# A conditioned mixture-of-experts layer: the gate folded into the second layer, the shared expert's turns deferred, and the pages' first layer with the expert's weights as stationary operand

## Chip, cores and metric

The kernel runs on one core of a Trainium2 chip. The metric is the device time of one execution in microseconds; the time before is the median of three runs. A profiled execution of the same kernel gives the span (first to last instruction) and everything that is read from the profile.

## What is computed

`x` has 8 batches of 512 tokens of 256 float32 numbers, here called tokens throughout. The reference, cut to what matters (`_ln` is a layer norm with gain and offset):

```python
h = _ln(x, pw_g[pathway], pw_b[pathway])            # gain and offset gathered by token
h = _ln(h, cp_g[compartment], cp_b[compartment])
t = _ln(x, tm_g[time], tm_b[time])
m, n, r = (x + mlp_ln(state) for each of three states of the batch)
s = _ln(x, ms_g[scale], ms_b[scale])
cat = concatenate([w[0]*h, w[1]*t, w[2]*m, w[3]*n, w[4]*r, w[5]*s])     # 6 x 256
xf = _ln(silu(cat @ int_W1 + int_b1) @ int_W2 + int_b2, int_g, int_be)  # 256
probs = softmax(xf @ gate_w.T)                      # 16 experts, the best 4 are used
moe = sum over the best 4 of p * (silu(xf @ w1[e].T) * (xf @ w3[e].T)) @ w2[e].T   # hidden width 128
shared = (silu(xf @ sw1.T) * (xf @ sw3.T)) @ sw2.T
out = x + moe + shared
```

## The kernel before

The work has two stages. **Stage 1** goes through the batches, each of 4 tiles of 128 tokens. Per batch: the gathers of `pw` rows and the first normalisation; transposes of x and of the normalised x (`turn_x`) and of h (`turn_h`); factors that select a class's gain by a product with a one-hot matrix (`factor`); the first layer into `ph` (`hidden`, L744 to L757, two halves of 128 hidden numbers, four sources in the order of the list HIDDEN) and its silu (`hidden_a`); the second layer into `pz` (`raw`, L766 to L780, two tiles in one PSUM buffer); statistics straight from PSUM (`raw_d`, `z_stats`); then

- `z_norm` (L803): ScalarE normalises from PSUM into `z`, tokens on the partitions;
- `z_turn` and `z_turn_a` (L807, L819): TensorE transposes z, ScalarE applies the norm's gain and offset and writes `xf` with the features on the partitions;
- `gate` (L827): xf tiles are the stationary operand, the 16 gate columns stream;
- `choose` (L840): VectorE takes the four largest of 16 logits; `rank` (L859): TensorE counts each token's place within its expert; `place` (L882): VectorE makes slot numbers from that;
- `scatter` (L946): one indirect DMA from GpSimd for each tile and each of the four choices writes rows of z into their slots of `xs_d` in HBM;
- `shared_1` and `shared_2` (L599 to L628): the shared expert from xf, with silu on ScalarE and a product and an addition to `x_all` on VectorE.

The last batch does the steps from `z_norm` to `place` in two groups of two tiles. `page_owners` and `page_experts` (L968 to L989) then find the expert of each page.

**Stage 2** goes through 143 pages of 128 slots each, sorted by expert, in 72 pairs (loop L1333 to L1362). For pair i: `load` brings four pages at a time from `xs_d`; `turn` (L1243, matmuls at L1250) transposes the pages, and ScalarE applies gain and offset (L1255); `first` (L1265): each page's transposed tokens are the stationary operand and the expert's w1 and w3, 256 columns at a place given by a register, stream (L1271); silu on ScalarE, product g on VectorE; `second_t` (L1283, matmuls at L1287) transposes g, VectorE copies it to `at`; `second` (L1295, L1304): at is stationary, w2 streams; ScalarE copies the result `yo`, and SP stores it into `ys_d`. `experts` (L1230) loads the numbers of four pages' experts into registers of TensorE. `fetch` (L1194) gathers results by slot from `ys_d` on GpSimd, at most two per pair; `weigh` adds them with their weights on VectorE, and `pick_weights` finds these weights during the first 32 pairs.

**What sets the order.** The class Plan (L61 to L126) is a list scheduler: every step is added with its engine, an estimated length, a rank, the steps that it follows, and slots that it takes and gives back (for instance two PSUM buffers each of the kinds t, h, m and o, three z buffers, six xf buffers). It writes each engine's order, which is then kept; the smallest rank that can start goes first. The shared expert has rank 400 plus its batch, so it fills what is left. GpSimd's transfers are kept in the program's order (`in_turn`), and scatters and gathers are paced by steps of VectorE (`in_time`). Stage 2's order is that of its loop. SP's order is that of the planned loads, then loads, stores and output of stage 2.

Of the kernel before, what the change touches and what calls it, by code (L numbers as in the profile page):

```python
# [18 lines left out]
P = 128  # L19
# [20 lines left out]
K_H, K_T, K_M, K_N, K_R, K_S = range(6)  # L40

F_B2, F_H, F_T, F_S = range(4)
F_X = F_B2
# [86 lines left out]
def adaln_ffn_kernel(ctx: ExitStack, tc: tile.TileContext, a: dict, out: bass.AP):  # L130
# [112 lines left out]
    iw2 = const.tile([P, NC, D], F32)  # L243
    gw = const.tile([P, NC, E], F32)
    ident = const.tile([P, P], F32)
# [18 lines left out]
    cls16 = const.tile([P, 4, D], BF16)  # L264
# [40 lines left out]

    iws = const.tile([P, 4, NC, D], F32)
    bias_t = const.tile([P, NC, B], F32)

    if True:
# [4 lines left out]
        def load_rest():  # L314
            nc.sync.dma_start(out=iw2, in_=a["int_W2"])
            nc.sync.dma_start(out=gw, in_=a["gate_w"])

# [48 lines left out]
        def halves(h):  # L366
            k = slice(F_T, F_S + 1) if h == 0 else slice(F_B2, F_H + 1)
            return cls16[:, k], second[:, k], tab[:, k]
# [38 lines left out]

        def gpsimd_tables():
            nc.gpsimd.memset(before, 1.0 / P)
# [46 lines left out]
        made = {}  # L456

# [141 lines left out]
    def shared_1(b, i):  # L599

        xf = res[b]["xf"]
        if i == 0:
            res[b]["act"] = p3.tile([P, S], F32, tag=tag("sact", "sh", b, 0), name=f"sact_{b}")
        ph = res[b]["sh", i] = ps_h.tile([P, S], F32, tag=tag("h", "sh", b, 0, i=i), name=f"sh{i}_{b}")
        for c in range(NC):
            nc.tensor.matmul(ph, s13[:, c, i], xf[:, c, :], start=(c == 0), stop=(c == NC - 1))  # L606
# [23 lines left out]
    with (  # L630
# [45 lines left out]
        def layer1_d(b, j):  # L676
# [4 lines left out]
            if "st_h" not in res[b]:  # L681
                res[b]["st_h"] = p2.tile([P, NJ, 6], F32, tag="st_h", name=f"st_h_{b}", bufs=B)
# [59 lines left out]
        HIDDEN = (F_T, F_S, F_X, F_H)  # L742

        def hidden(b, m, q):  # L744

            k = HIDDEN[q]
            cols = slice(m * P, (m + 1) * P)
            if q == 0:
                if m == 0:
                    res[b]["hid"] = p2.tile([P, NC, S], F32, tag=tag("hid", "hid", b, 0, 0), name=f"hid_{b}")  # L750
                res[b]["ph", m] = ps_h.tile([P, S], F32, tag=tag("h", "hid", b, m, 0), name=f"ph_{b}_{m}")
# [9 lines left out]
        def hidden_a(b, m):  # L761
            nc.scalar.activation(  # L762
# [3 lines left out]
        def raw(b, jj):  # L766

            hid = res[b]["hid"]
            if jj == 0:
                res[b]["z"] = p2.tile([P, NJ, D], F32, tag=tag("z", "raw", b, 0), name=f"z_{b}")  # L770
                res[b]["st_z"] = p2.tile([P, NJ, 6], F32, tag="st_z", name=f"st_z_{b}", bufs=B)
            pz = res[b]["pz", jj] = ps_o.tile([P, 2, D], F32, tag=tag("o", "raw", b, jj), name=f"pz_{b}_{jj}")
            for i in range(2):
                j = 2 * jj + i
                js = slice(j * P, (j + 1) * P)
                nc.tensor.matmul(
                    pz[:, i, :], hot_t[b][0:KCLS, js], cls16[0:KCLS, F_B2, :], start=True, stop=False
                )
                for m in range(NC):
                    nc.tensor.matmul(  # L780
                        pz[:, i, :], hid[:, m, js], iw2[:, m, :], start=False, stop=(m == NC - 1)
                    )

        def raw_d(b, jj):
            for i in range(2):
                vector.bn_stats(res[b]["st_z"][:, 2 * jj + i, :], res[b]["pz", jj][:, i, :])
# [16 lines left out]
        def z_norm(b, g, j):  # L803
            rs, nb = res[b]["zn", g]
            normalize(res[b]["z"][:, j, :], res[b]["pz", j // 2][:, j % 2, :], rs, nb, j - tiles_of(b, g)[0])
# [21 lines left out]
        def gate(b, g):  # L827
            xf, js = res[b]["xf"], tiles_of(b, g)
            pg = res[b]["pg", g] = ps_m.tile([P, len(js), E], F32, tag=tag("m", "gate", b, g), name=f"pg_{b}_{g}")
            for i, j in enumerate(js):  # L830
                for c in range(NC):
                    nc.tensor.matmul(  # L832
                        pg[:, i, :],
                        xf[:, c, j * P : (j + 1) * P],
                        gw[:, c, :],
                        start=(c == 0),
                        stop=(c == NC - 1),
                    )

        def choose(b, g):  # L840
# [4 lines left out]
            vector.tensor_copy(lx[:, js_, 0:E], res[b]["pg", g])  # L845
# [35 lines left out]

        def place(b, g):  # L882
# [4 lines left out]
            pr, mask = res[b]["pr", g], mask_all[:, b, js_]  # L887
# [5 lines left out]


            up = t("up")
            vector.tensor_scalar(up, pr[:, n:], 0.5 - 0.5 / P, ROUND, ALU.add, ALU.add)
            vector.tensor_scalar_add(end1, up, -ROUND)
# [33 lines left out]
            vector.tensor_tensor(pos, pr[:, 0:n], end0, ALU.is_ge)  # L931
            vector.tensor_mul(pos, pos, step)
            vector.tensor_add(pos, pos, pr[:, 0:n])
# [12 lines left out]
        def scatter(b, j, k):  # L946
# [3 lines left out]
                in_=res[b]["z"][:, j, :],  # L950
# [79 lines left out]
        add("rest", on="SP", took=0.9, rank=-94, lag=land, do=load_rest)  # L1030
# [6 lines left out]
        add("open", on="SP", took=0, rank=60, after=[("bias", 0), ("bias", 1), ("sca", 2), ("fill", 2)] + [("wown", i) for i in range(3)], do=open_weights)  # L1037
# [29 lines left out]
        add("wx", on="POOL", took=5, rank=-2, after=[("wsoft",), ("int", 1)], do=setup_x)  # L1067
        add("s1", on="PE", took=2, rank=-4, takes=["m"], after=[("st",)], do=states_1)
# [13 lines left out]
        for b in range(B):  # L1082
# [14 lines left out]
            for k in (F_T, F_S, F_H):  # L1097
                for c in range(NC):
# [7 lines left out]
                        gives=[("m", ("f", b, k, c))], do=factor_d)  # L1106
# [7 lines left out]
            for m in range(NC):  # L1114
                for q, k in enumerate(HIDDEN):
# [4 lines left out]
                    gives = {F_T: ("cat", ("f", b, F_T, 0)), F_S: ("cat", ("f", b, F_S, 0)), F_X: ("catx", ("tx", b, 0)), F_H: ("cath", ("f", b, F_H, 0))}  # L1120
                    add("hid", b, m, q, on="PE", took=1.75 + 0.22 * (k == F_H), rank=t + 20 + 7 * m, after=need,
                        takes=(["h"] + ["hid"] * (m == 0)) * (q == 0), gives=[gives[k]] * m, lag=0.12 if q == 3 else 0.0, do=hidden)
                add("hida", b, m, on="ACT", took=0.6, rank=t + 20 + 7 * m, after=[("hid", b, m, 3), ("bias", m)], gives=[("h", ("hid", b, m, 0))], do=hidden_a)
            for jj in range(2):
                add("raw", b, jj, on="PE", took=1.95, rank=t + 35 + jj, after=[("hida", b, m) for m in range(NC)] + [("begun", ("raw", b, 0))] * jj,
                    takes=["o"] + ["z"] * (jj == 0), gives=[("hid", ("hid", b, 0, 0)), ("hot", ("ht", b))] * jj, do=raw)
                add("rawd", b, jj, on="DVE", took=0.9, rank=t + 35 + jj, after=[("raw", b, jj)], do=raw_d)
            GROUPS = range(2 if b == B - 1 else 1)
            for g in GROUPS:
                js = tiles_of(b, g)  # L1130
                part = len(js) / NJ
                add("zs", b, g, on="DVE", took=2.4, rank=t + 26, after=[("rawd", b, j // 2) for j in js[::2]], do=z_stats)
                for j in js:
                    add("zn", b, g, j, on="ACT", took=0.49, rank=t + 27 + 0.1 * j, after=[("zs", b, g)], gives=[("o", ("raw", b, j // 2))] * (j % 2), do=z_norm)
                for c in range(NC):
                    add("zt", b, g, c, on="PE", took=0.44 * part, rank=t + 29 + c, after=[("zn", b, g, j) for j in js] + [("begun", ("zt", b, 0, 0))] * (c + g > 0),
                        takes=["t"] + ["xf"] * (c + g == 0), do=z_turn)
                    add("xf", b, g, c, on="ACT", took=0.2 + 0.48 * part, rank=t + 29 + c, after=[("zt", b, g, c)], gives=[("t", ("zt", b, g, c))], do=z_turn_a)
                add("gate", b, g, on="PE", took=1.8 * part, rank=t + 32, after=[("xf", b, g, c) for c in range(NC)], takes=["m"], do=gate)
                add("ch", b, g, on="DVE", took=0.5 + 1.6 * part, rank=t + 33, after=[("gate", b, g), ("tables",)], gives=[("m", ("gate", b, g))], do=choose)  # L1140
                add("rank", b, g, on="PE", took=0.5, rank=t + 34, after=[("ch", b, g), ("tables",)] + ([("pl", b, 0)] if g else [("pl", b - 1, 0)] if b else []), takes=["m"], do=rank)
                add("pl", b, g, on="DVE", took=4.0 + 2.2 * part, rank=t + 34, after=[("rank", b, g)] + [("po", (b - 4) // 2)] * (b >= 4), gives=[("m", ("rank", b, g))], lag=0.6, do=place)
                for j in js:
                    for k in range(TOPK):
                        add("sc", b, j, k, on="POOL", took=POOL_STEP, rank=t + 50 + 0.1 * j + 0.01 * k, after=[("pl", b, g), ("fill", b)],
                            gives=[("z", ("raw", b, 0))] * ((j, k) == (NJ - 1, TOPK - 1)), lag=2.3, do=scatter)
            for i in range(2):
                add("sh", b, i, on="PE", took=1.72, rank=400 + b, after=[("begun", ("sh", b, 0))] * i + [("xf", b, g, c) for g in GROUPS for c in range(NC)] + [("sw",)],
                    takes=["h", "h", "sact"] * (i == 0), do=shared_1)
            add("sha", b, on="ACT", took=0.6, rank=t + 50, after=[("sh", b, 0)], do=shared_1a)  # L1150
            add("shd", b, on="DVE", took=0.6, rank=t + 51, after=[("sha", b), ("sh", b, 1)], gives=[("h", ("sh", b, 0))], do=shared_1d)
            for jj in range(2):
                add("so", b, jj, on="PE", took=0.86, rank=400.5 + b, after=[("shd", b)] + [("begun", ("so", b, 0))] * jj, takes=["o"],
                    gives=[("xf", ("zt", b, 0, 0)), ("sact", ("sh", b, 0))] * (jj == 1), do=shared_2)
                add("sod", b, jj, on="DVE", took=0.68, rank=t + 60, after=[("so", b, jj)], gives=[("o", ("so", b, jj))], do=shared_2d)
# [67 lines left out]

    def load(q):
# [196 lines left out]
```

## Time and profile before

| what | us |
|---|---|
| median of three runs (555.72 to 556.39) | 555.81 |
| profiled execution, its own time | 556.97 |
| its span | 555.3 |
| TensorE busy | 512.4 |
| VectorE busy | 376.9 |
| GpSimd busy | 294.8 |
| ScalarE busy | 256.7 |
| first raw of batch 0 begins | 54.74 |
| last raw of batch 7 ends, about | 256.8 |
| last scatter begins | 297.25 |
| first transposes of the pages begin | 305.60 |
| a pair of pages, start to start | 3.25 |

Times within the profile are counted from the start of the span. PE is TensorE's matmuls and PEld its loads of the stationary operand, which overlap the matmuls; DVE is VectorE, ACT ScalarE, POOL GpSimd, SP the engine that issues most DMAs. A line of the timeline gives the start, the time from the first start to the last end, the engine, the source line, the operation with its output and inputs, and in brackets the idle time before it with what ended it. VectorE's operations go through a helper and all carry L139.

### The profile page before, as it was taken

The page shows a single profiled execution, that of the slowest core. Times are in us where ns is not written, and L with a number is a line of the kernel's source. Part 1 is how long each engine was busy: PE and PEld are TensorE (multiplying, and loading weights), DVE is VectorE, ACT ScalarE, POOL GpSimd, SP SyncE. Part 2 cuts the span into 40 slices and gives each one's busy share as a digit, 9 for nine tenths or more (in the row PEclk, how much of TensorE's full clock was granted, in tenths as well). Part 3 has the DMA queues.
Part 4 walks back from the last instruction along what each step waited for, and adds up shares of the span by engine and source line. Part 5 has one row for each costly group of instructions (what it writes and reads, how often), then busy time and mean ns, then how long its engine had stood idle before and what let it go on. Part 6 is the DMA issues. An engine that isn't in the chain of part 4 may idle for free.

```text
span 555.3 us, 8874 instructions
## 1 busy us (share of the span) xinstructions
PE 512.4 (92%) x2487; PEld 368.5 (66%) x2487; DVE 376.9 (68%) x1469; ACT 256.7 (46%) x509; POOL 294.8 (53%) x319
## 2 busy tenths in 40 slices
PE   3899999999989999998888999999999999999980
PEld 2446656554646555655545888888888888888860
DVE  8889889897868989857663534566664454455452
ACT  5552734451615532322102655655565556556640
POOL 7602207656656667575673002555655566665663
PEclk9998999998989999999899999999999999999995
DMA  6975657962879356646224355788888898888764
GB/s 220 368 215 157 185 169 211 259 205 94 264 224 301 122 161 220 182 152 224 87 104 158 108 173 169 220 292 264 264 257 260 249 273 280 262 261 254 225 200 120
DMA packets 107612, 116.83 MB, mean 210 GB/s; under 512 B 8744, under 2 KB 95141, under 8 KB 107565
## 3 DMA queue, kind: packets, MB, share of 16 engines
q1 hardware_dynamic: 92398, 74.26, 42.8%
q0 software_dynamic: 14848, 41.96, 24.9%
q8 instruction: 21, 0.34, 0.3%
q14 instruction: 26, 0.21, 0.1%
q10 hardware_dynamic: 319, 0.05, 0.1%
HBM read 57.78 MB, written 58.46 MB: 209 GB/s over the span
## 4 chain that ended last, share of the span: by engine, by line
PE 80%; DVE 11%; ACT 3%; DMA 3%; issue 2%; POOL 1%; POOLq 0%; DVEq 0%
PE hp L1271 22%; PE ph L757 17%; PE yo L1304 11%; PE xt L1250 6%; PE sh L606 4%; PE pz L780 3%; PE so L622 3%; PE pa L1287 3%; PE pg L832 2%; PE ptx L705 2%; PE pf L716 2%; DMA pw<-in_pw_dram,idx 1%; PE pth L732 1%; DVE cat L139 1%; PE p_table L395 1%
## 5 line engine op out<-in xcount | busy, mean ns | idle before, releaser
L1198 POOL DMA_INDIRECT yg<-ys_d,slot_all x128 | 124.1, 970 | 125.8 <-ACT yo L1308 43.5
L947 POOL DMA_INDIRECT xs_d<-z,slot_all x128 | 126.3, 986 | 78.0 <-issue 22.2
L1271 PE MATMUL hp<-w,xtt 128*128 x572 | 135.5, 380 | 0.2 <-ACT xtt L1255 0.2
L1271 PEld LDWEIGHTS hp<-w,xtt 128*128 128x128 f32 x572 | 103.1, 190 | 11.6 <-ACT xtt L1255 0.6
L139 DVE TENSOR_TENSOR g<-g,hp 128x256 f32<-128x256 f32 x72 | 30.2, 419 | 103.7 <-ACT g L1279 103.7
L757 PE MATMUL ph<-cat,iws 128*128 128x512 f32 x192 | 92.8, 613 | 0.0
L1255 ACT ACTIVATE xtt<-xt,vecs 128x256 f32<-128x256 f32 x144 | 73.2, 560 | 3.0 <-PE xt L1250 2.8
L1304 PE MATMUL yo<-w,at 128*128 x286 | 73.7, 380 | 0.0
L139 DVE SCALAR_TENSOR_TENSOR x_all<-yg,wk_all,x_all 128x256 f32<-128x256 f32 x128 | 59.0, 478 | 9.0 <-DMA yg<-ys_d,slot_all 7.9
L1308 ACT COPY yo<-yo 128x512 f32<-128x512 f32 x72 | 41.9, 583 | 49.7 <-PE yo L1304 46.2
L757 PEld LDWEIGHTS ph<-cat,iws 128*128 128x128 f32 x192 | 35.8, 195 | 34.6 <-issue 31.9
L639 POOL DMA_INDIRECT pw<-in_pw_dram,idx x32 | 31.1, 971 | 46.2 <-ACT cat L740 17.3
L1304 PEld LDWEIGHTS yo<-w,at 128*128 128x128 f32 x286 | 48.7, 190 | 4.1 <-issue 0.5
L1279 ACT ACTIVATE g<-hp 128x256 f32<-128x256 f32 x72 | 27.5, 383 | 44.9 <-PE hp L1271 44.9
L762 ACT ACTIVATE hid<-ph,bias_t 128x512 f32<-128x512 f32 x16 | 11.0, 688 | 70.8 <-PE ph L757 64.7
L1250 PE MATMUL xt<-ident,xs 128*128 128x128 f32 x286 | 42.8, 273 | 0.0
L1250 PEld LDWEIGHTS xt<-ident,xs 128*128 128x128 f32 x286 | 35.7, 141 | 7.0
L757 PE MATMUL ph<-catx,iws 128*128 128x512 f32 x64 | 32.5, 631 | 0.0
L780 PE MATMUL pz<-iw,hid 128*128 128x256 f32 x128 | 32.0, 378 | 0.0
L139 DVE COPY at<-pa 128x256 f32<-128x256 f32 x72 | 29.9, 415 | 0.0
L606 PE MATMUL sh<-xf,s 128*128 128x512 f32 x64 | 29.3, 597 | 0.0
L1287 PE MATMUL pa<-ident,g 128*128 128x128 f32 x143 | 27.4, 273 | 0.0
(195 smaller groups left out, 713.1 us busy)
## 6 DMA issues: line engine op xcount, KB each, us to landing
ys_d<-yo SPq DMA_DIRECT2D x71, 256.0 KB, 2.9
xs<-xs_d SPq DMA_DIRECT2D x35, 512.0 KB, 5.0
xs_d<-zero SPq DMA_DIRECT2D x8, 2048.0 KB, 12.5
x_all<-in_x_dram SPq DMA_DIRECT2D x8, 512.0 KB, 9.6
w<-in_w_dram SPq DMA_DIRECT2D x32, 128.0 KB, 5.9
out_dram<-x_all SPq DMA_DIRECT2D x32, 128.0 KB, 3.4
xs_d<-z,slot_all POOLq DMA_INDIRECT x128, 2.4
w<-in_w_dram SPq DMA_DIRECT2D x4, 512.0 KB, 6.7
```

The lines of the kernel that those rows point to most:

```text
L139: i = getattr(nc.vector, op)(*args, **kwargs)
L606: nc.tensor.matmul(ph, s13[:, c, i], xf[:, c, :], start=(c == 0), stop=(c == NC - 1))
L757: nc.tensor.matmul(res[b]["ph", m], l, r, start=(q == 0 and i == 0), stop=(q == 3 and i == len(mm) - 1))
L780: nc.tensor.matmul(pz[:, i, :], hid[:, m, js], iw2[:, m, :], start=False, stop=(m == NC - 1))
L947: i = nc.gpsimd.indirect_dma_start(out=xs_d[0 : pages_for(b, j) * P, :], out_offset=bass.IndirectOffsetOnAxis(ap=slot_all[:, b, j, k : k + ...
L1198: nc.gpsimd.indirect_dma_start(out=yg, out_offset=None, in_=ys_d[0:rows_, :], in_offset=bass.IndirectOffsetOnAxis(ap=slot_all[:, b, j, k : ...
L1250: nc.tensor.transpose(pt[:, c, k, :], src[:, p % QUAD, c * P : (c + 1) * P], ident)
L1255: a_ = nc.scalar.activation(xt[:, c, 0:n], pt[:, c, 0:n], AF.Identity, scale=vecs[:, V_INT_G, c : c + 1], bias=vecs[:, V_INT_BE, c : c + 1],)
L1271: nc.tensor.matmul(ph[:, k].rearrange("p i h -> p (i h)"), xt[:, c, k, :], w13[:, c, bass.ds(v, 2 * HID)], start=(c == 0), stop=(c == NC - 1),
L1287: nc.tensor.transpose(pa[:, k, :], g[:, k, :], ident)
L1304: nc.tensor.matmul(po[:, k, :], at[:, k, :], w2[:, bass.ds(v, D)], start=True, stop=True)
L1308: nc.scalar.copy(yo[:, o : o + n], po[:, 0:n])
```

## The change

**In stage 1** the gate's product becomes part of the second layer. With z the second layer's output before its norm, r the norm's reciprocal deviation, G the gate's matrix with the norm's gain multiplied in and its mean over the features taken off, the logits are r·(z·G) + int_be·gate. So `iw2` and the tables of int_b2 get 16 more columns (256 to 272). A setup of 24 TensorE passes makes them, with small steps on VectorE and ScalarE and one memset on GpSimd; `raw` waits for it. `raw` now writes one PSUM buffer per tile, ScalarE copies all 272 columns into z (`raw_a`), and `z_norm` works in place in SBUF. `choose` multiplies the 16 columns by r and adds the constant. The step `gate` is gone, and choose, rank, place no longer follow z_norm, z_turn and xf. The two reads of rank's result leave `place` and become steps of their own (`rank_d`, `rank_a` on ScalarE). `z_turn` goes from rank t+29 to t+38, the shared expert's ScalarE and VectorE steps get ranks 175 to 177, and its two PSUM buffers are taken and given back one at a time. The sources of the first layer have another order from batch 1 on. On SP, the load of gate_w goes ahead of int_W2, and a load of int_b2 in 256 pieces of four bytes follows.

**In stage 2** `first` makes the expert's weights the stationary operand and streams the 128 tokens, so that its output already has the hidden numbers on the partitions: `second_t` and the copy to at are gone. Since the weights' place depends on a register, they are copied first to a fixed buffer `wb` of 128x512 float32 for each page, by ScalarE for the first page of a pair and by VectorE for the second, two pairs ahead, three buffers each. `experts` loads the numbers into registers of TensorE, ScalarE and VectorE. `turn` runs two pairs ahead, `first` uses four PSUM buffers, `second` follows one step after `first`, and `yo` has a buffer per pair. The number of stores, fetches and weighings is the same.

In the order that results, TensorE does the shared expert of batch 0 ahead of raw of batch 7 (its last part just before it), and the other seven after it, with the second product of one batch between the first products of the next ones; the last turns of z come after rank of the last group. On VectorE the first two copies of weights follow the last addition of the shared expert.

```diff
-    iw2 = const.tile([P, NC, D], F32)
+    iw2 = const.tile([P, NC, DE], F32)
...
+        def gate_mean():
...
+        def gate_behind():
+            pt = made["gb"] = ps_o.tile([P, NC, E], F32, tag=tag("o", "gb"), name="p_gate")
+            for m in range(NC):
+                for c in range(NC):
+                    nc.tensor.matmul(
+                        pt[:, m],
+                        made["iw2_t"][:, c, m * P : (m + 1) * P],
+                        made["gates"][:, c],
...
+        def hidden_order(b):
+            return (F_T, F_X, F_S, F_H) if b else (F_T, F_S, F_X, F_H)
...
+        def raw_a(b, j):
+            nc.scalar.copy(res[b]["z"][:, j, :], res[b]["pz", j])
...
-        def gate(b, g):
...
         def choose(b, g):
-            vector.tensor_copy(lx[:, js_, 0:E], res[b]["pg", g])
+            rs = res[b]["zn", g][0]
+            shape = [P, len(js), E]
+            lx_ = lx[:, js_, 0:E]
+            vector.tensor_mul(lx_, res[b]["z"][:, js_, D:DE], rs.unsqueeze(2).to_broadcast(shape))
+            vector.tensor_add(lx_, lx_, gate_be.unsqueeze(1).to_broadcast(shape))
...
-                add("gate", b, g, on="PE", took=1.8 * part, rank=t + 32, after=[("xf", b, g, c) for c in range(NC)], takes=["m"], do=gate)
...
+    def bring_weights(i):
+        for k, p in enumerate(pages_of(i)):
+            v = values[p // QUAD, bring[k]][p % QUAD]
+            brought[p] = g2.tile([P, NC, 2 * HID], F32, tag=f"wb{k}", name=f"wb_{p}", bufs=3)
+            src = weights["w13"][:, :, bass.ds(v, 2 * HID)]
+            if bring[k] == ACT:
+                nc.scalar.copy(brought[p], src)
+            else:
+                vector.tensor_copy(brought[p], src)
...
     def first(i, xt):
...
-            for c in range(NC):
-                nc.tensor.matmul(
-                    ph[:, k].rearrange("p i h -> p (i h)"),
-                    xt[:, c, k, :],
-                    w13[:, c, bass.ds(v, 2 * HID)],
...
+            for h in range(2):
+                for c in range(NC):
+                    nc.tensor.matmul(
+                        ph[:, h, k, :],
+                        brought[p][:, c, h * HID : (h + 1) * HID],
+                        xt[:, c, k, :],
...
-    def second_t(i, g):
...
-            nc.tensor.transpose(pa[:, k, :], g[:, k, :], ident)
-        at = g2.tile([P, 2, P], F32, tag="at", name=f"at_{i}")
-        vector.tensor_copy(at[:, 0:n], pa[:, 0:n])
...
             nc.tensor.matmul(
-                po[:, k, :], at[:, k, :], w2[:, bass.ds(v, D)], start=True, stop=True
+                po[:, k, :], g[:, k, :], w2[:, bass.ds(v, D)], start=True, stop=True
...
     for i in range(n_pair + 2):
...
-        for t in (0, 1) if i == 0 else (i + 1,):
+        for t in range(3) if i == 0 else (i + 2,):
             if t < n_pair:
                 xt[t] = turn(t)
...
+        if i + 2 < n_pair:
+            bring_weights(i + 2)
```

## The prediction, on record before the changed kernel ran

> **What bounds the kernel now.** I read the page's busy row, slices and chain first, then the windows of its stages, then the page stage instruction by instruction. The busy row:
>
> ```profile
> PE 512.4 (92%) x2487; PEld 368.5 (66%) x2487; DVE 376.9 (68%) x1469; ACT 256.7 (46%) x509; POOL 294.8 (53%) x319
> ...
> PE 80%; DVE 11%; ACT 3%; DMA 3%; issue 2%; POOL 1%; POOLq 0%; DVEq 0%
> ```
>
> TensorE is busy 92% of the span and holds 80% of the chain that ended last. Work taken from it is worth time, unless a feeder stands close behind. That is read from three windows (span, then busy us of PE, PEld, DVE, ACT, POOL): steady batches, the seam from the last raw to the first page, pages.
>
> ```profile
> 54.70:256.60 201.90, 195.81 (x893) 118.08 (x892) 170.26 (x796) 84.03 (x153) 117.96 (x121) 0.98 0.66 202
> 256.60:305.60 49.00, 41.11 (x147) 24.29 (x146) 29.56 (x122) 9.37 (x16) 29.59 (x30) 0.93 0.33 116
> 305.60:538.20 232.60, 232.38 (x1286) 202.74 (x1284) 124.63 (x364) 137.09 (x287) 116.96 (x121) 1.00 0.77 236
> ```
>
> In the pages TensorE is never free. In the steady batches it waits 6 us of 202, but VectorE has 170 us of busy time in small operations, and all its listed waits sum to about 15 us: a second bound close behind. In the seam TensorE misses 8 us. One pair of pages, from the timeline (start, duration):
>
> ```profile
> 402.53 1.89 PE L1271 MATMUL hp<-w,xtt 128*128 x8
> ...
> 404.26 0.38 PE L1287 MATMUL pa<-ident,g 128*128 128x128 f32 x2
> ...
> 404.48 1.03 PE L1304 MATMUL yo<-w,at 128*128 x4
> ...
> 405.34 0.60 PE L1250 MATMUL xt<-ident,xs 128*128 128x128 f32 x4
> ...
> 405.78 1.89 PE L1271 MATMUL hp<-w,xtt 128*128 x8
> ```
>
> Read starts, not durations [...]. hp 8 passes 1.73 us (0.216 each), pa 2 in 0.22 (0.110), yo 4 in 0.86 (0.215), xt 4 in 0.44 (0.110): 3.25 us a pair. A float32 product is two passes. The gate, and the wait that follows z_turn in the last batch (bracket: idle time before it, and its releaser):
>
> ```profile
> 68.22 1.85 PE L832 MATMUL pg<-gw,xf 128*128 128x16 f32 x16
> 69.92 1.96 PE L757 MATMUL ph<-catx,iws 128*128 128x512 f32 x4
> ```
> ```profile
> 261.22 0.60 PE L813 MATMUL pxf<-ident,z 128*128 128x128 f32 x4
> 263.77 0.90 PE L813 MATMUL pxf<-ident,z 128*128 128x128 f32 x4 [1.95 <-ACT xf L819]
> 264.51 1.86 PE L832 MATMUL pg<-gw,xf 128*128 128x16 f32 x16
> ```
>
> The gate takes 1.70 us for 16 passes, 0.106 each, though only 16 columns stream: it pays for its stationary operands.
>
> **What the Trainium skill says.** (1) "TensorE: Matmul & The Clock Gate", section "LDWEIGHTS (loading the stationary operand)": a load costs its columns over 1.2 ns, 107 ns for 128, whatever streams. The gate's 106 ns agrees. (2) Same page, "Wait — 56ns, not 53.3ns?": about 2.5 ns fixed per matmul on top of the stream. 216 ns for 256 columns and 110 for 128 fit two cycles of 2.4 GHz per column plus 2.5. (3) "SBUF — State Buffer", section "Who interferes with whom": a VectorE copy in its two-port mode and GpSimd lock each other out of a shared port pair. The page stage has no such copy today (at is read from PSUM), so no row of before shows it. (4) Price: "VectorE: DVE Perf Modes", "The perf-mode tier table": 1227 ns for a float32 SBUF copy of 2048 elements a row; less a fixed part, I estimate 0.42 us for 512 (ends 0.33 and 0.68, the latter a 128x512 two-operand row of this trace). No run shows it.
>
> **Pages.** Removed from TensorE per pair: pa, 0.22. Changed: hp becomes 16 passes of 128 columns, each with its own 128-column load. The nearest row is xt, a 128-column pass with a fresh 128x128 float32 load, at 0.110: 16×0.110 = 1.76 against 1.73. So 0.44+1.76+0.86 = 3.06 against 3.25, −0.19×71.5 pairs = −13.6. Bounds of a pass: 0.107 (a bare load or stream) and 0.190, the recorded load time, if loads stop hiding; I take 0.110, because the xt row already does exactly this back to back.
> What hides the new work: ScalarE per pair xtt 1.02, yo 0.58, silu 0.38 (both already there), new copy of a page's weights 0.59 (the row xn or catx of 128x512), new register load 0.17 (TensorE's took 0.33 per two pairs; bounds 0 to 0.33): 2.74 < 3.06. VectorE: g mul 0.42, weigh 0.96, picks 0.67 (first 32 pairs), new copy 0.42, new register load 0.17, less at 0.42: 2.64, bounded by 2.4 and by 3.6 if each copy also waits out a 0.97 us GpSimd step. GpSimd two fetches of 1.275 = 2.55, plus up to 0.42 of lockout: 2.97. All just under 3.06, so cover is thin: without it the pair stays near 3.25. The copies look two pairs ahead with three buffers, so a single late one costs nothing; if they fall behind for good, hp waits for them, and behind hp in TensorE's queue wait the last pair's yo and the next xt, so everything slips. The same 72 stores go through SP's queue (their bytes don't change), and the fetches keep their pace of two a pair on GpSimd's. DMA share goes from about 0.86 to 0.92 by the shorter period. The first pair waits for VectorE's first copies, queued behind the last shared additions: +0.5 (0 to 1.5). Pages −13.1.
>
> **Head.** The fold costs 24 passes (mean 8, iw2 transposes 4, product 8, b2 4), 2.6 us at 0.107, ahead of raw(0), and two loads change place on SP with one of 256 four-byte pieces; raw waits for gba and g2d, and behind a waiting raw stand the hidden passes of batch 1. The small VectorE and ScalarE steps sit between other setup. I take +3 (1.6 if only the passes count, 5 with a wait of 2.4 for the folded columns).
>
> **Steady batches.** TensorE loses 7 gates, −7×1.70 = −11.9, and one shared expert but one half, −4.3 (it moves to the seam). It gains 16 columns in raw: 4 float32 passes of 13 ns and one of 7 per tile, 32 tiles, +1.9. Sum −14.3. VectorE's work hardly changes (shared adds −1.4, choose's two ops of 0.23 for one of 0.22, +1.7), so its floor is its waits, about −14 of 202. ScalarE gains 32 PSUM copies of 0.42, 84 to 97 us of 190, hidden. GpSimd must place 148 steps of 1.275, 189 us, between its first scatter and the last. The scatters start earlier by the removed normalise, turn and gate (first one 82 before, about 75 after). The moved turns keep a z slot (three) until turn and scatters are both done, and the deferred shared work keeps xf slots (six): that is why batch 0's shared work must still run ahead of raw(7). I cost both at nothing: the last scatter of a batch outlives its turn, and six slots last to batch 6; if a slot were late, raw of that batch would wait, up to the 1.2 us that a wait for raw shows today. None of the three engines leaves more than 14; small waits always remain: I take −11 (−5 to −14).
>
> **Seam.** Two chains. TensorE after raw(7): 7 shared experts of 5.17 = 36.2, turns and ranks 2.1: 38.3, plus waits. Today each so waits 0.85 for sact as below; the change interleaves so of one batch with sh of the next, so 1.5 to 3 remain: 40 to 42 against 49.
>
> ```profile
> 297.49 1.99 PE L622 MATMUL so<-s,sact 128*128 128x256 f32 x8 [0.85 <-DVE sact L139]
> ...
> 303.77 1.99 PE L622 MATMUL so<-s,sact 128*128 128x256 f32 x8 [0.85 <-DVE sact L139]
> 305.60 0.60 PE L1250 MATMUL xt<-ident,xs 128*128 128x128 f32 x4
> ```
>
> The slots: from raw(7)'s second tile (254.8) to the end of place today 20.7 us. Off that chain go the turn, its wait and the gate (261.22 to 266.21, 5.0) and two normalises (1.2) with what queued between, about −7: 13.6. Then 16 scatter steps to the start of the last (+19 to 20.4), 2.56 to the load's issue (297.25 to 299.81 today) and 5.0 to its landing: 41 to 42 after 254.8, where today stands 50.8. Both chains end near 42: −7 (−3 to −10).
>
> **Sum.** +3 −11 −7 −13.1 = −28.1. Span 555.3 → 527.2; the profiled execution's 556.97 lies 1.67 outside its span: 528.9; it ran 1.16 above the median 555.81: 527.7.
>
> **Rivals.**
> R1, a feeder holds stage 1: VectorE or the scatter queue gives back most of it, steady −3 and seam −3. For: VectorE is busy or between small operations 187 of 202 us. Against: its waits include the gate's own (lg_all on pg 3.8 us). +3−3−3−13.1 = −16.1, 539.7.
> R2, the pages stay at 3.25: ScalarE or VectorE becomes the bound by register loads, copies and the shared port. For: 2.74 and 2.97 of 3.06. Against: no queue exceeds 3.06 on its middle price. 540.8. With R1 too, 552.8.
> R3, slower, one mechanism: the 128-column streams don't cover their loads in hp, and each pass costs the recorded load time, 190 ns (row PEld of hp). Place: L1271's successor. Price: 16×0.080 = 1.28 a pair, +91.5: 619.2. It decides from 135 ns a pass, where 16×0.0246×71.5 = 28.1 eats the whole gain. For: PEld is busy 203 of 233 us already. Against: xt at 0.110 with loads recorded at 141, and the gate at 0.106 with float32 loads: recorded loads overlap.
> That the change doesn't do what it says is excluded for TensorE: the planned order has no gate and no second turn; whether the shared work fills the seam's gaps is R1's question.
>
> **How the numbers follow.** Forecast 0.58 (518 to 537 by its own terms); R1 0.16; R2 0.12; R1 and R2 together 0.02; R3 0.07; a larger gain, under 513, if the seam and steady terms reach their far ends, 0.05. The range 513 to 545 holds the forecast, R1 and R2, 0.86, and leaves out the rest. A measurement tells about 0.2% from no change: faster 0.92, same 0.01, slower 0.07.
>
> **What would show it.** hp 1144 passes, starts 0.110 apart, pairs 3.06 apart, no pa, no pg; first xt near 290 instead of 305.6; raw(0) near 57.7; so without its 0.85; ScalarE's weight copy near 0.59, VectorE's near 0.42. I am wrong if TensorE waits for wb in the pages, if hp passes stand 0.13 or more apart, or if VectorE's waits vanish while TensorE's grow in the steady batches.

## The result, and the profile after

The changed kernel takes 547.52 us (median; 546.25 to 550.27), the kernel before 555.86 beside it: ratio 0.9855, 95% interval 0.9814 to 0.9896. It is 8.3 us faster, where 28.1 were forecast and the forecast range ended at 545. The profiled execution has a span of 546.5 us, 8.8 less than before. In 14 of the 18 later runs the kernel before itself took 603 to 616 us, with gaps on all engines that no kernel explains, so their times decide nothing and what their traces show behind the second raw is an indication at most.

The page of the changed kernel: its busy row, its chain and three groups (busy us and mean ns of one; idle before):

```profile
PE 492.3 (90%) x2812; PEld 363.7 (67%) x2812; DVE 386.3 (71%) x1488; ACT 306.5 (56%) x625; POOL 294.9 (54%) x320
...
PE 66%; DVE 22%; ACT 5%; DMA 3%; issue 2%; POOL 0%; ACTq 0%; DVEq 0%; SPq 0%; POOLq 0%
...
L1383 PE MATMUL hp<-xtt,wb 128*128 128x128 f32 x1144 | 139.5, 275 | 0.0
...
L1345 ACT COPY wb<-w 128x512 f32 x72 | 44.7, 622 | 0.0
...
L141 DVE COPY wb<-w 128x512 f32 x71 | 31.3, 443 | 3.9 <-issue 2.8
```

TensorE lost 20 us of work, and its share of the chain fell from 80 to 66% while VectorE's rose from 11 to 22%: steps of VectorE now end waits that were not there. Where they lie is read from the windows of the same stages (head, first to last raw, seam, pages):

```profile
0.00:59.12 59.12, 46.04 (x189) 27.61 (x190) 50.90 (x200) 26.66 (x56) 22.89 (x42) 0.94 0.73 233
59.12:261.92 202.80, 183.75 (x768) 103.10 (x767) 169.96 (x794) 95.33 (x189) 120.93 (x124) 0.98 0.65 197
261.92:308.57 46.65, 41.07 (x142) 22.99 (x141) 32.08 (x125) 11.75 (x22) 25.29 (x26) 0.96 0.39 136
308.57:530.70 222.13, 221.42 (x1717) 210.01 (x1715) 128.94 (x361) 172.37 (x358) 118.89 (x121) 1.00 0.80 245
```

| stage | before | after | difference | forecast |
|---|---|---|---|---|
| head, to the first raw | 54.74 | 59.12 | +4.4 | +3 |
| first to last raw | 202.06 | 202.80 | +0.7 | −11 |
| seam, to the first page | 48.80 | 46.65 | −2.2 | −7 |
| pages and tail | 249.7 | 237.9 | −11.8 | −13.1 |

The second line is the surprise: TensorE's busy time there fell by 12.2 (195.97 to 183.75), and its idle time rose by 13.0 (6.1 to 19.05). VectorE's idle time there stayed nearly as it was, 31.7 us before and 32.8 after. The pages did what they were meant to do. One pair:

```profile
402.23 0.60 PE L1359 MATMUL xt<-ident,xs 128*128 128x128 f32 x4
...
402.66 1.95 PE L1383 MATMUL hp<-xtt,wb 128*128 128x128 f32 x16
...
404.45 1.03 PE L1403 MATMUL yo<-w,g 128*128 x4
...
405.31 0.60 PE L1359 MATMUL xt<-ident,xs 128*128 128x128 f32 x4
```

16 passes from 402.66 to 404.45: 0.112 each. The pair takes 3.08 (3.09 in most), not 3.25, and TensorE is busy 221.4 of 222.1 us.

**Where TensorE waits between the raws.** From the first raw of one batch to that of the next there are seven intervals. Three of them, those that end at raw of batches 2, 4 and 5, hold 17.5 of the 19.05 us of idle time:

```profile
83.55:118.31 34.76, 30.32 (x118) 15.93 (x117) 30.75 (x156) 15.43 (x31) 24.48 (x26) 0.95 0.81 245
143.62:175.43 31.81, 25.55 (x110) 13.89 (x109) 27.86 (x133) 14.27 (x29) 20.99 (x23) 1.00 0.77 231
175.43:210.15 34.72, 27.91 (x118) 15.04 (x117) 30.80 (x142) 16.91 (x34) 23.94 (x25) 0.95 0.71 209
```

The waits of TensorE from 59.1 to 261.9 (total, times, longest):

```profile
PE ph L839 <- DVE cat L141: 5.5, 2, 3.3
PE pf L798 <- DVE cat L141: 3.3, 3, 2.9
PE pz L858 <- DVE st_z L141: 2.8, 4, 1.2
PE pxf L894 <- ACT catx L790: 1.8, 2, 1.1
PE pxf L894 <- ACT cat L822: 1.7, 1, 1.7
```

8.8 us are waits for cat, VectorE's products of the next batch's factors (1.5 in the kernel before). Three waits, one in each of these intervals, make up nearly all of it: 2.91 at 104.62, 2.24 at 164.40, 3.29 at 196.68. The first, on TensorE:

```profile
99.83 1.88 PE L839 MATMUL ph<-catx,iws 128*128 128x512 f32 x4
104.62 0.38 PE L798 MATMUL pf<-hot_t,cls 72*128 72x512 bf16 x1 [2.91 <-DVE cat L141]
104.83 2.59 PE L839 MATMUL ph<-cat,iws 128*128 128x512 f32 x4
```

and on VectorE just before it:

```profile
103.11 0.41 DVE L141 MAX8 top_all<-pos_all 128x8 f32<-128x16 f32 x4
...
103.81 0.17 DVE L141 COPY shifts<-shifts 128x16 f32<-128x16 f32 x1
103.89 0.68 DVE L141 TENSOR_TENSOR cat<-cat,pf 128x512 f32<-128x512 f32 x1
104.48 0.68 DVE L141 TENSOR_TENSOR cat<-catx,pf 128x512 f32<-128x512 f32 x1
105.10 0.69 DVE L141 TENSOR_TENSOR cat<-cat,pf 128x512 f32<-128x512 f32 x1
```

top_all and the copy of shifts are the end of `place` of batch 1, one step of the plan and 6.3 us long (97.71 to 103.98). The three cat that follow belong to batch 2 and had to stand behind it. In the order of before, place of batch b comes after all six cat of batch b+1, for b from 1 to 5; there place could not start before the turn and the gate were done. In the changed order choose and place are ready earlier, and the planner put place of batches 1, 3 and 4 ahead of the last two or three cat of the next batch: just the batches whose first layer then waits (2, 4 and 5). By rank it prefers place: in the changed plan place has 33 where the last two cat of the next batch have 36 and 37. The wait of 2.91 us was followed by a half clock (granted 0.50 from 106.5 to 108.5): the four passes at 104.83 end 2.59 later, where others of this kind take 1.88. The wait of 3.29 was followed by one too, the wait of 2.24 was not.

### The profile page after: what moved, and what is told of

Read it like the earlier page. It is cut to its first block, busy times and chain, and to the rows that moved or that the text cites. A ratio compares the mean times of both kernels' runs of the same rounds, so it can differ in the third digit from the quotient of the medians.

```text
span 546.5 us, 9591 instructions
## 1 busy us (share of the span) xinstructions
PE 492.3 (90%) x2812; PEld 363.7 (67%) x2812; DVE 386.3 (71%) x1488; ACT 306.5 (56%) x625; POOL 294.9 (54%) x320
## 4 chain that ended last, share of the span: by engine, by line
PE 66%; DVE 22%; ACT 5%; DMA 3%; issue 2%; POOL 0%; ACTq 0%; DVEq 0%; SPq 0%; POOLq 0%
PE hp L1383 23%; PE ph L839 11%; PE yo L1403 11%; PE xt L1359 6%; PE sh L688 3%; PE so L704 2%; PE pz L860 2%; ACT z L749 2%; DVE pw L141 2%; DVE cat L141 2%; DVE sums L141 2%; DVE ru_z L141 1%; DMA yg<-ys_d,slot_all 1%; DVE st_z L141 1%; DVE rs_z L141 1%
## 5 line engine op out<-in xcount | busy, mean ns | idle before, releaser
L1383 PE MATMUL hp<-xtt,wb 128*128 128x128 f32 x1144 | 139.5, 275 | 0.0
L1383 PEld LDWEIGHTS hp<-xtt,wb 128*128 128x128 f32 x1144 | 133.6, 192 | 0.1
L839 PE MATMUL ph<-cat,iws 128*128 128x512 f32 x192 | 95.7, 621 | 6.4 <-DVE cat L141 5.5
L1403 PE MATMUL yo<-w,g 128*128 x286 | 73.7, 381 | 0.0
L1403 PEld LDWEIGHTS yo<-w,g 128*128 128x128 f32 x286 | 48.9, 191 | 3.9 <-DVE g L141 0.2
L1345 ACT COPY wb<-w 128x512 f32 x72 | 44.7, 622 | 0.0
L1391 ACT ACTIVATE g<-hp 128x256 f32<-128x256 f32 x72 | 27.5, 382 | 14.6 <-PE hp L1383 14.1
L860 PE MATMUL pz<-iw,hid 128*128 128x272 f32 x128 | 34.7, 393 | 0.4 <-ACT hid L846 0.4
L141 DVE COPY wb<-w 128x512 f32 x71 | 31.3, 443 | 3.9 <-issue 2.8
L688 PE MATMUL sh<-xf,s 128*128 128x512 f32 x64 | 31.2, 623 | 2.7 <-ACT sact L692 2.7
L839 PE MATMUL ph<-catx,iws 128*128 128x512 f32 x64 | 30.2, 594 | 0.0
```

The source lines that it names most:

```text
L141: i = getattr(nc.vector, op)(*args, **kwargs)
L839: nc.tensor.matmul(res[b]["ph", m], l, r, start=(q == 0 and i == 0), stop=(q == 3 and i == len(mm) - 1))
L860: nc.tensor.matmul(pz, hid[:, m, js], iw2[:, m, :], start=False, stop=(m == NC - 1))
L1345: nc.scalar.copy(brought[p], src)
L1383: nc.tensor.matmul(ph[:, h, k, :], brought[p][:, c, h * HID : (h + 1) * HID], xt[:, c, k, :], start=(c == 0), stop=(c == NC - 1),)
L1403: nc.tensor.matmul(po[:, k, :], g[:, k, :], w2[:, bass.ds(v, D)], start=True, stop=True)
```

## The experiments

Four theories say why the steady batches didn't gain. V: the amount of VectorE's work bounds them (rival R1 of the prediction). H: hand-overs do, since a PSUM tile must be emptied by one engine before TensorE fills it again. W: the changed pages hurt stage 1. And later O: the order does, with cat behind place on VectorE.

**Halves of the change.** Stage 1 of one kernel joined to stage 2 of the other, no other edit. Stage 2 new alone:

> Stage 2 of the changed kernel on stage 1 of the kernel before, nothing else. Both theories: the pages are independent of stage 1, so all of their gain shows: pair period 3.09 us instead of 3.25, first transposes of the pages near 305.6 as before (plus some 0.5), time 544 to 546. If instead the page gain needs the changed stage 1, about 550.

Measured 617.67 beside 615.2, and again:

> Stage 1 of before with the pages of the changed kernel: pair period 3.09 us from 305.6 on, 11 us less than before: 543 to 546, faster than the whole change. If the page gain needs the changed stage 1: 550 or more.

607.97 beside 602.99. Stage 1 new alone:

> Stage 1 of the changed kernel with the pages of before. Theory V (VectorE is the bound of stage 1, so TensorE's removed gate buys nothing and the longer head stays): 557 to 560, slower than before. Rival W (the changed pages hurt stage 1, by early loads or transfers): 545 to 552, the promised gain of the fold appears.

> Stage 1 of the changed kernel with the pages of before. Theory V and rival H alike (the fold's gain is lost inside stage 1): 556 to 560, first transposes of the pages near 308.5, slower than before. Rival W (the changed pages hurt stage 1): 545 to 552.

> Stage 1 of the changed kernel with the pages of before. All theories that place the loss inside stage 1: first transposes of the pages near 308.5 as in the changed kernel, then 233 us of pages as before: 556 to 561, no faster than before. If the changed pages hurt stage 1: 545 to 552.

614.96 beside 615.2, 607.40 beside 602.82, 606.71 beside 602.99. The times say nothing on the forecasts. What can be used: the first raw comes at 52.4 and 52.8 us in pages_only and at 57.5, 57.9 and 59.6 in stage1_only, so the head's cost belongs to the new stage 1, with a size that is uncertain by some 2 us, as the same code spread by so much; from the first raw to the second stage1_only takes 24.4 us, as the whole change does (24.43). On W there is an indication: with the old pages, too, the intervals that end at raw of batches 2, 4 and 5 are long (38.7, 34.4 and 36.3 us in stage1_only_c), while the one that ends at batch 6 takes 24.29, as in the whole change; the one that ends at batch 3 is longer as well (31.5 against 25.3). The loss then sits in the new stage 1. In pages_only pairs without a gap are 3.09 apart: the page gain doesn't need the new stage 1. That the two parts add up was not shown.

**The gate's work put back, in an order of the planner's own.**

```diff
+    add("dg", b, g, on="PE", took=1.8 * part, rank=t + 38 + NC, after=[("xf", b, g, c) for c in range(NC)], takes=["m"], gives=[("m", ("dg", b, g))], do=dead_gate)
```

> The changed kernel, with the old gate's matmuls put back as dead work: 16 passes of 16 columns a batch, behind the batch's turns, into a buffer that nobody reads; 13.6 us of TensorE in all, 11.9 of it between the first and the last raw. Theory V (VectorE bounds the steady batches, TensorE has 19 us to spare there): the time rises by no more than 3 us over the changed kernel's 547.5, to 546 to 551. Rival H (TensorE's own queue with its hand-overs is still the bound): the time rises by 8 to 12, to 556 to 560.

Measured 564.22 beside 554.92, ratio 1.0169 (1.0118 to 1.0220): 17 over the changed kernel, beyond both theories, for 13.6 us of work. Its window from first to last raw, and the largest of VectorE's waits (the line counts the whole run; the wait of 14.0 lies in this window):

```profile
59.06:277.33 218.27, 204.44 (x888) 120.96 (x887) 169.99 (x794) 96.39 (x190) 126.50 (x130) 0.96 0.62 189
```
```profile
DVE sact L141 <- PE sh L688: 18.4, 5, 14.0
```

TensorE's busy time grew by 20.7 there, more than the dead work (a mean clock of 0.96 against 0.98 and eight more passes of the shared expert are part of it), and VectorE stood 14.0 us in one wait for the shared expert: the planner, given one step more, had made another order of every engine. So the run tells nothing of V and H. It shows that an added step isn't a test of one cost where a planner lays out the rest. The dead work then went inside an existing step, so that all engines keep their order:

```diff
 def z_turn(b, g, c):
+    for i in range(len(js)):
+        nc.tensor.matmul(pt[:, i * E : (i + 1) * E], iws[:, 0, c, 0:P], gw[:, c, :], start=True, stop=True)
```

> The changed kernel with the gate's 128 passes of 16 columns put back as dead work inside the turns of z, on constant operands, into a buffer that the turns then overwrite. No step, rank or order changes (the first try had let the planner make another order of all engines). 13.6 us of TensorE in all, 11.9 of it between the first and the last raw, behind nothing but the turns. Theory V (VectorE bounds the steady batches): at most 3 us over the changed kernel's 547.5, so up to 551. Rival H (TensorE's queue with its hand-overs is the bound): 8 to 14 us over it, 556 to 561.

> The changed kernel in its own order, with the gate's 128 passes of 16 columns put back as dead work inside the turns of z (13.6 us of TensorE, 11.9 of it between first and last raw), as before, when the kernel before took 603 us beside it. Theory V: at most 3 us over the changed kernel's 547.5. Theory O and rival H (TensorE stands in the chain of every interval, because each engine's order makes it wait and then hurry): 7 to 13 us over it, 554 to 561.

621.40 beside 602.82 and 620.14 beside 602.99. Readable is the first interval of raws, which holds one dead gate of 1.70 us: 25.63 both times (58.58 to 84.21, 59.08 to 84.71) against 24.43. 1.20 of 1.70 shows there. That speaks against V in that interval; it has no wait for cat behind place, so it tells nothing of O.

**VectorE lightened, in the same order.** VectorE finds each reciprocal deviation by three Newton steps of three small operations each; this variant leaves two of them out.

```diff
-        for _ in range(3):
+        for _ in range(1):
```

> The changed kernel with one Newton step instead of three in each reciprocal deviation: it leaves out two steps of refinement, 6 VectorE operations of about 0.195 us at each of 22 places, 25.7 us of VectorE in stage 1, of which about 20 between the first and the last raw; the order of all work is the same. Theory V: the steady batches shrink by 12 to 18 us (until TensorE's 184 us there bound), time 528 to 536. Rival H (VectorE isn't short of time, but every step waits for a hand-over of one PSUM tile between TensorE, ScalarE and VectorE): only the two-step shortening of the chain counts, at most 5 us, 542 to 547.

> The changed kernel with one Newton step instead of three in each reciprocal deviation, run again because the kernel before itself took 615 us beside the first try. It leaves out two steps of refinement, 6 VectorE operations of about 0.195 us at each of 22 places, 25.7 us of VectorE in stage 1, of which about 20 between the first and the last raw; the order of all work is the same. Theory V: the steady batches shrink by 12 to 18 us (until TensorE's 184 us there bound), time 528 to 536. Rival H (VectorE isn't short of time, but every step waits for a hand-over of one PSUM tile between TensorE, ScalarE and VectorE): only the two-step shortening of the chain counts, at most 5 us, 542 to 547.

> The changed kernel with one Newton step instead of three in each reciprocal deviation (two steps of refinement left out), as twice before, when the kernel before took 615 us beside it. 25.7 us of VectorE go from stage 1, 20 of them between the first and the last raw, with the same order. Theory V: 12 to 18 us less in the steady batches, 528 to 536. Rival H: at most 5 us from a shorter chain, 542 to 547.

> The changed kernel with one Newton step instead of three in each reciprocal deviation (two steps of refinement left out, 25.7 us of VectorE in stage 1, 20 of them between the first and the last raw, same order), as before, when the kernel before took over 600 us beside it. Theory V (VectorE's serial work bounds the steady batches): 10 to 18 us less than the changed kernel's 547.5, so 529 to 538, and TensorE's waits for cat and for the PSUM tiles of raw shrink by about as much. Rival H (hand-overs of single tiles and TensorE's own queue bound): at most 5 us less, 542 to 547.

These four took 615.53, 614.02, 610.01 and 614.14 beside 615.2, 616.42, 602.82 and 607.88, and decide nothing. The fifth:

> The changed kernel with one Newton step instead of three (two steps of refinement left out, 25.7 us of VectorE in stage 1), in the unchanged order; four earlier tries ran beside a kernel before that took 603 to 615 us. Theory V: 8 to 16 us less than the changed kernel, 531 to 539. Rival H: at most 5 us less, 542 to 547.

Measured 536.78 beside 555.72, ratio 0.9648 (0.9615 to 0.9681), 10.7 less than the changed kernel. This is V's number, but by luck, since it does not come from V's place. First to last raw, and TensorE's two largest waits in it:

```profile
52.48:251.86 199.38, 185.81 (x768) 104.14 (x767) 156.30 (x706) 95.14 (x189) 121.35 (x124) 0.97 0.67 203
```
```profile
PE ph L839 <- DVE cat L141: 5.5, 2, 3.3
PE pf L798 <- DVE cat L141: 2.9, 1, 2.9
```

The stretch lost 3.4 us (202.8 to 199.4), though VectorE's busy time fell by 13.7; its idle time rose by 10.2 instead (32.8 to 43.1). Of the rest 6.6 came from the head (first raw at 52.48; it lies between 52.1 and 55.8 in the five traces of this kernel), 0.6 from the seam. The waits for cat stayed at 5.5 and 2.9, as long as before. They don't depend on how much VectorE has to do, but on what stands between: rank on TensorE, then place, then cat. VectorE's first read of rank's result for batch 1 (up, pr), in the changed kernel and here, and the end of TensorE's wait here:

```profile
96.31 0.22 DVE L141 TENSOR_SCALAR up<-pr 128x64 f32<-128x64 f32 x1 [0.68 <-PE pr L948]
```
```profile
88.68 0.23 DVE L141 TENSOR_SCALAR up<-pr 128x64 f32<-128x64 f32 x1 [1.58 <-PE pr L948]
...
96.98 0.59 PE L798 MATMUL pf<-hot_t,cls 72*128 72x512 bf16 x1 [2.90 <-DVE cat L141]
```

The lighter VectorE only waits longer for rank, 1.58 us instead of 0.68; from there to the end of TensorE's wait 8.3 us pass in both (96.31 to 104.62, 88.68 to 96.98). V falls for this order. The same edit in the kernel before:

> The same two Newton steps left out of the kernel before. Theory V: TensorE is busy 196 of 202 us there, so the steady batches can gain at most 6 us, head and seam 2 to 5 more: 545 to 552, clearly less than in the changed kernel. Rival H: the same small gain as in the changed kernel, or more.

> The same two Newton steps left out of the kernel before. Theory V: TensorE is busy 196 of 202 us in the steady batches, so at most 6 us there and 2 to 5 in head and seam: 545 to 552. Rival H: as small a gain as in the changed kernel, or more.

606.91 beside 615.2 and 599.02 beside 602.82: of no use.

**A new order.** One Newton step less, the shorter steps told to the planner, and its slack 0.1 us instead of 0.3. Among the steps that can start within the slack of the earliest one, the planner takes the smallest rank:

```diff
-    LAG, SLACK, SHARE = 0.12, 0.3, 0.0
+    LAG, SLACK, SHARE = 0.12, 0.1, 0.0
...
-        for _ in range(3):
+        for _ in range(2):
...
-                add("zs", b, g, on="DVE", took=2.4, rank=t + 26, after=[("rawd", b, j) for j in js], do=z_stats)
+                add("zs", b, g, on="DVE", took=1.81, rank=t + 26, after=[("rawd", b, j) for j in js], do=z_stats)
```

> The changed kernel with two Newton steps instead of three in each reciprocal deviation (one step of refinement left out: 3 VectorE operations of 0.195 us at 22 places, 12.9 us, some 10 between the first and the last raw), the planner told of the shorter steps and its slack set from 0.3 to 0.1 us, so that it makes an order for the lighter VectorE. Theory V (VectorE's serial work and its place in the order bound the steady batches): the stretch from first to last raw falls from 202.8 to 184 to 190 us, TensorE's listed waits there from 18 to under 6, time 522 to 532. Rival H (hand-overs of single PSUM tiles, which this version keeps): at most 5 us less, 542 to 547.

Measured 527.51 beside 555.72, ratio 0.9492 (0.9471 to 0.9513): 20 less than the changed kernel. First to last raw and seam, then TensorE's largest wait between the raws:

```profile
55.71:241.00 185.29, 179.78 (x764) 102.67 (x762) 160.79 (x747) 93.04 (x188) 114.19 (x117) 1.00 0.69 210
241.00:288.44 47.44, 39.27 (x146) 24.03 (x145) 32.44 (x122) 12.73 (x23) 32.12 (x33) 0.96 0.37 132
```
```profile
PE pf L798 <- DVE cat L141: 3.4, 4, 2.2
```

185.3 instead of 202.8. TensorE idles 5.5 instead of 19.05 us; the waits of ph for cat are gone, and in this order place stands behind all six cat of the next batch again, for batches 1 to 5. VectorE has more work here than in after_n1_e (160.79 us against 156.30), and yet the stretch is 14.1 us shorter (185.29 against 199.38), 8.1 of it idle time of TensorE: most of the rest a higher clock (1.00 against 0.97): the order makes this difference, not the amount. The V of this forecast already took in the place in the order; it is the comparison with after_n1_e that tells V and O apart. The PSUM tiles are handed over just as in the changed kernel, so H, which allowed 542 to 547, falls too. The stretch is 16.8 us shorter than before (202.06), but not all of this is the change's, as the same step left out of the kernel before shows:

> The same one Newton step left out of the kernel before, with the shorter steps told to its planner (slack as it was). Theory V: TensorE is the bound there, 196 of 202 us; the gain is what is left of its waits and a shorter head and seam, 2 to 8 us, so 548 to 554: less than half of what the changed kernel gains. Rival H: as much as in the changed kernel.

Measured 548.66 beside 555.72, ratio 0.9898 (0.9847 to 0.9948), 7.1 less. First to last raw 195.14, with TensorE busy 188.97:

```profile
51.32:246.46 195.14, 188.97 (x881) 114.74 (x880) 160.56 (x746) 82.27 (x150) 117.40 (x120) 1.00 0.67 206
```

TensorE bounds that kernel. Beside it, with the same step left out of both (the slack is lowered only in the changed one), the stretch is 9.9 us shorter, 185.29 against 195.14, where TensorE has 9.2 less to do (188.97 to 179.78): what TensorE is spared now shows as time. The whole change is worth 21.2 us in this pair (548.66 to 527.51), less than the 28.1 forecast. At last, the new order with all three Newton steps and nothing left out:

> The changed kernel in the order of after_n2_plan (527.5 us), with all three Newton steps: nothing is left out, only the order differs from the changed kernel's. It puts 22 times 3 VectorE operations of 0.195 us, 12.9 us, back, about 10 of them between the first and the last raw, where VectorE has about 7 us of idle time by that order. Theory V (VectorE's serial work bounds, in whatever order): 8 to 13 us above after_n2_plan, 535 to 541. Theory O (the order that the planner made, with cat behind place on VectorE, is what lost the gain; VectorE's work itself has room): at most 5 above it, 527 to 533, far below the changed kernel's 547.5.

602.42 beside 602.99: not decided by its time. Its first interval of raws is 25.07 (58.40 to 83.47) against 24.49 in after_n2_plan (55.71 to 80.20): 0.58 more, which is one Newton step (3 times 0.195). Further on its trace points to the order. From the first raw of the first batch to that of the last, here and in stage1_only_c, which has the same stage 1 in the changed kernel's order and was taken beside the same 602.99:

```profile
58.40:257.17 198.77, 181.78 (x744) 102.46 (x743) 165.04 (x781) 92.22 (x184) 111.05 (x114) 0.97 0.61 187
57.49:274.50 217.01, 186.13 (x749) 103.17 (x748) 168.82 (x790) 93.83 (x185) 118.47 (x121) 0.95 0.60 180
```

It is 18 us shorter with about the same work of VectorE, and TensorE idles 17.0 instead of 30.9 us; the other two traces of stage1_only have 215.5 and 219.8. With the gaps that these traces hold, this is an indication. How much of the 17.5 us the order keeps under the full VectorE work stays open.

## Why the prediction was wrong, step by step

**Pages: right.** The sum had 3.06 for a pair, measured 3.09; a pass costs 0.112 where 0.110 was taken, 16×0.002×71.5 = 2.3 us, more than the gap between −13.1 and −11.8. R2 and R3 didn't come: TensorE doesn't wait for wb, ScalarE's copy took 0.622 (0.59), VectorE's 0.443 (0.42, the estimate from the Trainium skill's "VectorE: DVE Perf Modes", section "The perf-mode tier table", which the run supports).

**Steady batches: the step that failed**, "None of the three engines leaves more than 14; small waits always remain: I take −11". TensorE's loss was sized well (−12.2 measured against −14.3). What I took for granted is that the small waits stay small when work leaves. I asked of each engine how much work it has, and not where in its fixed order the freed steps go. The gate and the turn were also a delay that kept place, 6.3 us in one piece, behind the next batch's cat; without it the planner moved place ahead, TensorE waited, and 13.0 us of idle time replaced 12.2 of work. Waits for cat are 7.3 of these 13.0; the rest is shorter waits, nearly all in the same three intervals, which were not taken apart. The trace shows the cause by position, after_n1_e shows that the waits don't shrink with VectorE's work, and after_n2_plan that those of the first layer go, and the gain appears, under an order with place behind. Of the signs of being wrong that the prediction named, TensorE's waits did grow in the steady batches, but VectorE's didn't vanish. R1 had named VectorE and the scatter queue, but by amount of work. Its 539.7 was still too hopeful, mostly because it kept −6 for steady and seam, where −1.5 was measured.

That place's position alone, with all work kept, gives back the whole 17.5 us was not shown: after_n2_plan changed VectorE's work and the order together, and a new plan moves other steps too. No run moved place alone.

**Seam: right mechanism, mis-sized.** The last scatter begins at 295.46 and TensorE ends the shared work at 308.57, so TensorE's chain decides. "1.5 to 3" us of waits were 5.6. Two were not in the sum:

```profile
270.04 3.50 PE L688 MATMUL sh<-xf,s 128*128 128x512 f32 x4 [2.49 <-ACT sact L692]
274.79 0.18 PE L948 MATMUL pr<-mask_all,before 128*128 128x32 bf16 x1 [1.25 <-DVE mask_all L141]
```
```profile
268.42 1.09 ACT L749 ACTIVATE z<-z,nb_z,rs_z 128x256 f32<-128x256 f32 x2 [2.47 <-DVE up L141]
269.41 0.57 ACT L692 ACTIVATE sact<-sh 128x512 f32<-128x512 f32 x1
```

The silu of a shared expert stands on ScalarE behind the normalise of the last group, which waits 2.47 us for VectorE; TensorE's next sh waits for the silu's buffer. After the idle time its four passes take 3.50 us instead of 1.88. 2.49+1.25+1.6 = 5.3, about the whole gap of 4.8.

**Head: mis-sized,** +4.4 against +3 (4.7 to 7.2 between the first raws of the halves). The folding passes lie before the first raw as forecast, and pb_state waits 1.61 us for vt and then runs at a lower clock, 4.22 us against 2.74 before.

## What to carry to other kernels

Where each engine has a fixed order, a removed step is also a removed delay: ask which long step becomes ready earlier, and in front of whose short, urgent step it now falls. Test with the order held fixed, since an added step lets a planner rearrange everything. Compare idle time by releaser before and after a change, not only the busy sums.

## What the runs showed of the hardware

Matmuls of 128 float32 columns with a new 128x128 float32 stationary operand each ran 0.112 us apart, 16 in a row in every pair of the 222 us of pages, though each load is recorded at 0.192.

After waits of TensorE of 2.91 and 3.29 us between the raws, and of 2.49 us in the seam, its granted clock was 0.50 for some 3 us. That is no rule of the wait's length: after one of 2.24 us it stayed at 1.00, and so it did after one of 3.23 us in before_n2_plan (at 116.23), while the kernel before had 0.50 from 126.6 to 129.9 with no wait of more than 1.0 us ahead.

The Trainium skill says in "SBUF — State Buffer", section "Who interferes with whom", that a VectorE copy in its two-port mode and GpSimd block each other. One of GpSimd's steps, 0.95 us as a rule, ran longer beside a copy of wb:

```profile
400.69 0.42 DVE L141 COPY wb<-w 128x512 f32 x1
400.72 1.21 POOL L1291 DMA_INDIRECT yg<-ys_d,slot_all  x1 [0.30 <-DVE x_all L141]
```

That the copy is the cause was not shown: the kernel before has a step of 1.21 us too (at 529.65), in pages without any such copy, and the mean of these steps is 982 ns after and 970 before. It cost nothing here, since GpSimd has 3.09 us for two steps.
